# Convolution in passes of 256 channels over half the blocks, W_glu loaded in slices, and the last result made in two parts

## The chip, the core and the metric

The kernel runs on one core of a Trainium2 chip. The metric is the device time of one execution in microseconds, as the median of three runs. A profile of one further execution gives the busy times, waits and DMA packets that the text reads. Engine names are those of the profile: PE is the matrix engine (PEld is its weight load), DVE the vector engine, ACT the scalar engine, POOL the GpSimd engine, SP the engine that issues most DMAs. A queue with a q at its end (SPq, ACTq, POOLq) stands for the DMA issues of that engine.

## The reference

There are two layers on an input x of 32 images, 128 channels and 32 x 32 pixels (1024 positions), all in float32.

The first layer is a state-space block. Its input is u, the group norm of x with groups of 4 channels. For each image it computes

- h = W_enc^T u + b_enc, which has 1024 channels,
- a causal convolution of each channel of h along the 1024 positions with a filter of 64 taps, which comes from the parameters of that channel, plus D times h; the result goes through gelu and is called y,
- g = y W_glu + b_glu, which has 2048 columns, and then the first half times the sigmoid of the second half,
- the layer norm of h + g over the 1024 channels, then W_dec, which brings it back to 128 channels.

The result is added to x and gives x1.

The second layer is a deformable convolution with 64 taps (8 x 8). A depthwise 3 x 3 convolution of the group norm of x1 gives an x and a y offset for every tap and pixel. Each tap samples the normed image bilinearly at its shifted place, every channel has a weight of its own for every tap, the sum over the taps goes through a batch norm and gelu, and it is added to x1.

## The kernel before

**Filter table.** `ssm_kernel_table` builds the filters of all 1024 channels and writes them to DRAM as `kp_d`, one row of 320 values per channel, of which 64 are taps and the others zero.

**Convolution stage** (`ssm_convolution`, L183 to L341). The positions of an image are cut into 8 blocks of 128. The stage makes 8 passes of 128 channels (the loop over k at the end). A pass has two parts.

`encode(k)` makes z for all 32 images. For each image it loads u (512 KB, L236; in the first pass it makes u by the group norm of x and stores it with an ACT DMA), and does two groups of 4 matmuls that give 128 positions x 128 channels each (L223). The bias is added by DVE on the way out of PSUM (L227, 128 x 512), with a write that is strided by channel. Two PSUM buffers (`psz`) take turns.

`convolve(k, z)` takes 8 channels at a time, 16 times. For them it loads `toe` with SP (L281): 128 partitions x 8 channels x 192 values, each partition one value further along the row of the filter, so that it holds a band matrix whose outer columns are zeros. The ring has three such tiles. For each of two halves (i) of the blocks and each channel, one matmul with z as weights (4 blocks x 32 images are its 128 rows) and toe as the moving operand gives 192 columns (L299). The 64 columns that run over into the next block are copied by ACT (`t`, L307) and added to the next block's rows by DVE (`carry`, L311); the last block of the first half is carried to the second half from the tile `last`. ACT applies gelu (L320) into a `yo` tile, of which there are six; POOL stores it to `y_d` with 8 DMAs of 128 KB per 8 channels (L332). The carry is followed by `finish()`, which issues the gelu or the stores of the step before. The order is written by hand (`manual_schedule`).

**Main block** (`main_block`). It takes over the on-chip memory of the convolution stage. It loads its constants with SP (L588) and all of W_glu (8 MB, eight ACT DMAs, L597), folds the layer norm's gamma and beta into W_dec (the matmuls of L625 and L637 and the DVE scaling of L632, all in `pdec`), and clears `rel_d` with four zero stores (L653). `first_part(b)` is the rest of the first layer for an image, in two halves of 512 positions: it loads y (`gy`, L677) and u, and for m from 0 to 7 does eight matmuls for the gate (L757), the sigmoid on ACT (L764), eight for the value (L780) and then h (L796). A tile (image and half) takes some 130 us when it is alone.

`second_part(b, steps)` is the sampling of an image. The taps and columns of the image are cut into 17 packs (`PACKS`) of up to 16 slots and each pack into 4 pieces of two filter rows. Per piece, SP loads hat functions in x (`ds`) and y (`dhy`) from DRAM (`load_hat`, L1029), DVE multiplies them (L1048), and three matmuls over the row ranges of `rows_of` (L1091, windows starting at rows 0, 8 and 16) sample the image. DVE multiplies by the tap weights (L1094), POOL or DVE adds the two filter rows (L1111), POOL adds into `acc` (L1116). A pack whose slots are not one run in DRAM needs several loads (`runs_of`): four for the first and the last pack, two for the second and the last but one. `steps` are pieces of work for the next image that are placed at given counts.

`run_along` merges `first_part(b + 2)` and `second_part(b)` in proportion to estimated costs. For the last two images (from `ALONE` on) there is no first part left; the hats in x are then loaded into 32 partitions only and spread by ACT copies (L1040).

**End.** After the last pack of an image, POOL takes off the mean and scales (L1122), ACT applies gelu (L1126), DVE adds x1 (L1127) and ACT issues the store (L1128). For the last image these four come after everything else. Then `deformable_redo` compares the largest offsets with `BOUND_X` and `BOUND_Y` (L1177 to L1194) and reads the outcome back: an image whose offsets are beyond the bound would be done again by `deformable_general`, a slow general path.

Of the kernel before, what the change touches and what calls it, by code (L numbers as in the profile page):

```python
# [14 lines left out]
P = 128  # L15
# [167 lines left out]
def ssm_convolution(nc, tc, const, ins, x, u_d, kp_d, y_d):  # L183
# [7 lines left out]

    ORDER = (0, 2, 1, 3)
    NB = NJ // 2
    RW = TW - P
    QC = 4
    with tc.tile_pool(name="cvt", bufs=3) as tp, tc.tile_pool(
        name="cvz", bufs=1
    ) as zp, tc.tile_pool(name="cv1", bufs=1) as one, tc.tile_pool(
        name="cvu", bufs=5
    ) as up, tc.tile_pool(name="cvy", bufs=6) as yp, tc.tile_pool(  # L200
# [7 lines left out]
        nc.sync.dma_start(b_enc, ins["b_enc_row"].to_broadcast([P, D]))  # L208

        def encode(k):  # L210

            z = [
                pool.tile([P, P, NB, B], F32, tag=f"z{g}", name=f"z_{k}_{g}")
                for g, pool in enumerate((one, zp))
            ]
            bias = b_enc[:, k * P : (k + 1) * P]

            def image(b, u):
                for g in range(2):
                    ps = psz.tile([P, NB, P], F32, tag="ps", name=f"psz_{k}_{b}_{g}")  # L220
                    for j in range(NB):
                        lo = (NB * g + ORDER[j]) * P
                        nc.tensor.matmul(  # L223
                            ps[:, j, :], u[:, lo : lo + P], w_enc[:, k * P : (k + 1) * P],
                            start=True, stop=True,
                        )
                    nc.vector.tensor_add(  # L227
                        z[g][:, :, :, b].rearrange("p d j -> p j d"),
                        ps,
                        bias[:, None, :].to_broadcast([P, NB, P]),  # L230
                    )

            if k > 0:
                for b in range(B):
                    u = up.tile([P, L], F32, tag="u", name=f"u_{k}_{b}")
                    nc.sync.dma_start(u, u_d[b])  # L236
                    image(b, u)
                return z
# [28 lines left out]
        def convolve(k, z):  # L267
            rows = [t.rearrange("p d j b -> p d (j b)") for t in z]
            waiting = []

            def finish():
                for work in waiting:
                    work()
                waiting.clear()

            for g in range(P // CG):
                d0 = k * P + g * CG
                toe = tp.tile([P, CG, TW], F32, tag="toe", name=f"toe_{d0}")
                table = kp_d[d0 : d0 + CG, 0:TW]

                nc.sync.dma_start(  # L281
                    toe,
                    bass.AP(
                        tensor=table.tensor,
                        offset=table.offset,
                        ap=[[1, P], [KPW, CG], [1, TW]],
                    ),
                )
                yo = [
                    yp.tile([P, CG, P], F32, tag="yo", name=f"yo_{d0}_{i}") for i in range(2)  # L290
                ]
                for q in range(CG // QC):
                    c0 = q * QC
                    last = None
                    for i in range(2):
                        ps = psy.tile([P, 2, 512], F32, tag="ps", name=f"psy_{d0}_{q}_{i}")
                        ps = ps[:, :, : 2 * TW].rearrange("p h (c n) -> p h c n", c=2)
                        for c in range(QC):
                            nc.tensor.matmul(  # L299
                                ps[:, c // 2, c % 2, :],  # L300
                                rows[i][:, g * CG + c0 + c, :],
                                toe[:, c0 + c, :],
                                start=True,
                                stop=True,
                            )
                        over = tp.tile([P, 2, 2, RW], F32, tag=f"t{i}", name=f"t_{d0}_{q}_{i}")
                        nc.scalar.copy(over, ps[:, :, :, :RW])  # L307

                        def carry(to, rows, src):
                            own = ps[to : to + rows, :, :, P:TW]  # L310
                            nc.vector.tensor_add(own, own, src)  # L311

                        carry(64, 64, over[0:64])
                        carry(32, 32, over[64:96])
                        if i > 0:
                            carry(0, 32, last[96:P])
                        finish()

                        def gelu(to=yo[i][:, c0 : c0 + QC, :], ps=ps):
                            nc.scalar.activation(  # L320
                                to.rearrange("p (h c) l -> p h c l", c=2),
                                ps[:, :, :, RW:TW][:, :, :, ::-1],
                                AF.Gelu_apprx_tanh,
                            )

                        waiting.append(gelu)
                        last = over

                def store(yo=yo, d0=d0):
                    for i in range(2):  # L330
                        for j in range(NB):
                            nc.gpsimd.dma_start(  # L332
                                y_d[d0 : d0 + CG, :, i * NB + ORDER[j], :].rearrange(
                                    "d b l -> b d l"
                                ),
                                yo[i][j * B : (j + 1) * B],
                            )

                waiting.append(store)
            finish()  # L340


        with tc.manual_schedule():
            for k in range(KD):
                convolve(k, encode(k))
# [156 lines left out]
BOUND_X, BOUND_Y = 2.45, 3.25  # L502
# [9 lines left out]
def rows_of(piece):  # L512

    a, b = 15 - KY2 * piece, 23 - KY2 * piece
    return (0, a), (a, b - a), (b, H - b)
# [30 lines left out]
def main_block(nc, tc, const, ins, x, u_d, y_d, x1_d, out, offmax):  # L546
# [21 lines left out]
    with ctx:  # L568
# [27 lines left out]
        for k in range(KD):  # L596
            nc.scalar.dma_start(w_glu[:, k, :], ins["W_glu"][k * P : (k + 1) * P, :])  # L597
# [13 lines left out]
        minus = constant("minus", [P, 16])  # L611
        off_w = constant("offset_w", [P, 9])
# [8 lines left out]


        fold = pdec.tile([P, T], F32, tag="dec", name="g_fold")
        for k in range(KD):
            nc.tensor.matmul(  # L625
                fold[:, 0:1], w_dec[:, k, :], beta[:, k : k + 1],
                start=(k == 0), stop=(k == KD - 1),
            )
        shift = one.tile([P, 1], F32, tag="shift", name="g_shift")
        nc.vector.tensor_add(shift, fold[:, 0:1], b_dec)  # L630
        for k in range(KD):
            nc.vector.tensor_scalar(  # L632
                w_dec[:, k, :], w_dec[:, k, :], gamma[:, k : k + 1], None, op0=ALU.mult
# [684 lines left out]
```

## Time and profile before

| | us |
|---|---|
| median of three runs (13580.38 to 13586.92) | 13584.75 |
| the profiled execution | 13588.92 |
| its span in the profile | 13587.2 |
| PE busy (96%) | 13106.8 |
| POOL busy (67%) | 9080.3 |
| DVE busy (65%) | 8781.8 |
| ACT busy (24%) | 3291.8 |
| psy matmuls L299, 4096 rows | 704.7 |
| psz matmuls L223, 4096 rows | 568.6 |
| DVE adds for z, L227, 512 | 516.2 |
| store issues for y_d on POOL, L332, 1024 | 590.1 |

A row of the page counts a float32 matmul twice, since it is done in two rows. Busy time of PE is not PE at its peak. The span is shorter than the execution's own time by what lies before its first and after its last instruction (1.7 us). The trace also has every DMA packet with its queue, size and time; a packet of 4096 B on the POOL queue is a piece of a store of y, one of 768 B on SP's queue in the convolution stage is a row of toe.

### The profile page before, as it was taken

Reading aid. Unit: us, or ns where it says so; the run is one execution under the profiler, and the core shown is the slowest. Engines: PE = TensorE matmul, PEld = TensorE weight load, DVE = VectorE, ACT = ScalarE, POOL = GpSimd, SP = SyncE. Lnnn points to the kernel's source line nnn. Section 1 sums busy time; section 2 is a strip of 40 time slices with the busy share of each in tenths; the row PEclk is TensorE's granted clock in tenths of the full one; section 3 lists DMA queues with packets and bytes.
Section 4 is the critical chain, followed back from the end, with each engine's and each line's share of the span. In section 5 each row is a group of like instructions: output and inputs, shape, how many; then the busy total and the mean of one; then the engine's idle time right before and its main releaser. Section 6 shows DMA issues by size and latency. Waiting matters only on the chain.

```text
span 13587.2 us, 133930 instructions
## 1 busy us (share of the span) xinstructions
PE 13106.8 (96%) x40482; PEld 7248.5 (53%) x40482; DVE 8781.8 (65%) x12685; ACT 3291.8 (24%) x4767; POOL 9080.3 (67%) x8868
## 2 busy tenths in 40 slices
PE   7999899999999999999999999999999999999975
PEld 7888545555555555555555555555555555555533
DVE  7787226666666666666666666666666666666677
ACT  4333222222211122222222211112222222221145
POOL 2444227777777777777777777777777777777778
PEclk9999999999999999999999999999999999999988
DMA  7888428888888888888889888888888888988876
GB/s 244 275 277 273 132 90 231 234 239 236 231 227 231 233 235 238 238 236 232 230 234 239 235 229 229 231 232 237 238 237 236 232 230 235 240 235 231 230 198 175
DMA packets 1715626, 3105.77 MB, mean 229 GB/s; under 512 B 308306, under 2 KB 1018322, under 8 KB 1713874
## 3 DMA queue, kind: packets, MB, share of 16 engines
q1 hardware_dynamic: 1502290, 2641.91, 73.2%
q10 hardware_dynamic: 163456, 320.92, 6.6%
q0 software_dynamic: 49152, 134.28, 2.9%
q8 instruction: 329, 5.39, 0.2%
q14 instruction: 399, 3.27, 0.1%
HBM read 2630.36 MB, written 466.06 MB: 228 GB/s over the span
## 4 chain that ended last, share of the span: by engine, by line
PE 81%; DMA 9%; DVE 4%; ACT 2%; POOL 2%; issue 1%; SPq 1%; ACTq 0%; DVEq 0%; POOLq 0%
PE gpv L780 24%; PE gpg L757 23%; PE dps L1091 23%; DMA ds<-dhat 4%; PE gph L796 3%; PE gpo L685 3%; PE psy L299 3%; PE psz L223 2%; DMA y_d<-yo 2%; DMA dhat<-dh 2%; DVE z L227 1%; DVE ds L1048 1%; DMA dhy<-dhat 1%; POOL y_d L332 1%; ACT ds L1040 0%
## 5 line engine op out<-in xcount | busy, mean ns | idle before, releaser
L1094 DVE TENSOR_TENSOR dp<-dps,k_weight_slots 128x256 f32<-128x256 f32 (+17 forms) x6528 | 3087.1, 483 | 3109.5 <-PE dps L1091 2914.8
L1091 PE MATMUL dps<-ds,dxw 128*128 128x256 f32 (+18 forms) x13056 | 4701.1, 447 | 223.5 <-DVE ds L1048 177.5
L1116 POOL TENSOR_TENSOR dacc<-dacc,dp 128x256 f32<-128x256 f32 (+3 forms) x4736 | 4417.4, 933 | 396.5 <-DVE dp L1111 26.6
L1091 PEld LDWEIGHTS dps<-ds,dxw 128*128 128x128 f32 x13056 | 2472.7, 192 | 3203.6 <-issue 2537.5
L757 PE MATMUL gpg<-gy,g_w_glu 128*128 128x512 f32 x8192 | 3986.4, 593 | 23.5 <-DMA gy<-y_d 15.7
L780 PE MATMUL gpv<-gy,g_w_glu 128*128 128x512 f32 x8192 | 3975.7, 592 | 0.0
L1111 POOL TENSOR_TENSOR dp<-dp 128x448 f32<-128x448 f32 (+2 forms) x2142 | 2675.1, 1249 | 1882.1 <-DVE dp L1094 1879.4
L1048 DVE TENSOR_TENSOR ds<-ds,dhy 128x1024 f32<-128x1024 f32 (+3 forms) x2176 | 3148.6, 1447 | 762.4 <-DMA ds<-dhat 647.9
L757 PEld LDWEIGHTS gpg<-gy,g_w_glu 128*128 128x128 f32 x8192 | 1546.9, 190 | 1235.8 <-issue 964.9
L780 PEld LDWEIGHTS gpv<-gy,g_w_glu 128*128 128x128 f32 x8192 | 1551.7, 190 | 1155.3 <-issue 913.8
L818 POOL TENSOR_TENSOR gs<-gs,gq 128x512 f32<-128x512 f32 x448 | 628.5, 1403 | 1341.3 <-ACT gq L817 1341.3
L817 ACT ACTIVATE gq<-gr 128x512 f32<-128x512 f32 x448 | 282.3, 630 | 4673.6 <-DVE gr L809 4611.2
L332 POOL DMA_DIRECT2D y_d<-yo x1024 | 590.1, 583 | 869.7 <-ACT yo L320 699.2
L764 ACT ACTIVATE gs<-gpg,k_b_glu 128x512 f32<-128x512 f32 x512 | 351.8, 687 | 2488.0 <-PE gpg L757 2377.6
L953 ACT ACTIVATE dh<-dr,k_minus 128x624 f32<-128x624 f32 x768 | 621.7, 809 | 642.5 <-DMA dhat<-dh 563.1
L299 PE MATMUL psy<-toe,z 128*128 128x192 f32 x4096 | 704.7, 333 | 45.2 <-ACT yo L320 43.8
L299 PEld LDWEIGHTS psy<-toe,z 128*128 128x128 f32 x4096 | 667.5, 192 | 81.6 <-ACT yo L320 74.5
L311 DVE TENSOR_TENSOR psy<-psy,t 32x256 f32<-32x256 f32 (+1 forms) x1280 | 553.7, 433 | 204.7 <-ACT t L307 162.6
L788 DVE SCALAR_TENSOR_TENSOR gs<-gpv,k_b_glu,gs 128x512 f32<-128x512 f32 x512 | 379.7, 742 | 437.3 <-PE gpv L780 437.2
L687 POOL TENSOR_TENSOR gs<-gs,gr 128x512 f32<-128x512 f32 x448 | 634.7, 1417 | 0.0
L954 ACT ACTIVATE dh<-dh,one 128x624 f32<-128x624 f32 x768 | 626.3, 815 | 25.0
L223 PE MATMUL psz<-w_enc,u 128*128 128x128 f32 x4096 | 568.6, 293 | 44.9 <-DVE z L227 32.3
(162 smaller groups left out, 6052.4 us busy)
## 6 DMA issues: line engine op xcount, KB each, us to landing
dhy<-dhat SPq DMA_DIRECT2D x1536, 512.0 KB
ds<-dhat SPq DMA_DIRECT2D x1440, 512.0 KB
dhat<-dh ACTq DMA_DIRECT2D x768, 312.0 KB
y_d<-yo POOLq DMA_DIRECT2D x1024, 128.0 KB, 5.4
gy<-y_d SPq DMA_DIRECT2D x512, 256.0 KB
u<-u_d SPq DMA_DIRECT2D x224, 512.0 KB
toe<-kp_d SPq DMA_DIRECT2D x128, 768.0 KB
dxw<-dvt_d SPq DMA_DIRECT2D x1248, 64.0 KB
```

Of the source, the lines that this page charges most:

```text
L223: nc.tensor.matmul(ps[:, j, :], u[:, lo : lo + P], w_enc[:, k * P : (k + 1) * P], start=True, stop=True,)
L299: nc.tensor.matmul(ps[:, c // 2, c % 2, :], rows[i][:, g * CG + c0 + c, :], toe[:, c0 + c, :], start=True, stop=True,)
L332: nc.gpsimd.dma_start(y_d[d0 : d0 + CG, :, i * NB + ORDER[j], :].rearrange("d b l -> b d l"), yo[i][j * B : (j + 1) * B],)
L687: nc.gpsimd.tensor_add(sums[0], sums[0], r)
L757: nc.tensor.matmul(gate, w_glu[:, k, D + m * P : D + m * P + P], ys[k], start=(k == 0), stop=(k == KD - 1),)
L780: nc.tensor.matmul(val, w_glu[:, k, m * P : m * P + P], ys[k], start=(k == 0), stop=(k == KD - 1),)
L818: nc.gpsimd.tensor_add(sums[1], sums[1], sq)
L1048: nc.vector.tensor_mul(s[:, :m], s[:, :m], hy[:, :m])
L1091: nc.tensor.matmul(ps, xw[:, j, :], s[:, :m, :, y0 : y0 + ny], start=True, stop=True)
L1094: nc.vector.tensor_mul(prod[:, :m, :, y0 : y0 + ny], ps, w[:, :, :, None].to_broadcast([P, m, KY2, ny]),)
L1111: adder.tensor_add(prod[:, :m, 0], prod[:, :m, 0], prod[:, :m, 1])
L1116: nc.gpsimd.tensor_add(to, to, prod[:, slot : slot + nj, 0])
```

## The change

- **Passes.** A pass has 256 channels (`ZC`) and half of the blocks; there are four passes over k with two halves each. `encode(k, half)` loads half of u per image (256 KB), does two groups of two matmuls with 256 columns, and, except in the very first pass, gives every fourth group to ACT (copy) and POOL (bias) in place of DVE.
- **Convolve.** One half per pass, 32 groups of 8 channels. The three toe tiles are static and are zeroed once; only the 128 columns that can be non-zero are loaded, by two DMAs of 64 partitions each. What runs over from the first half into the second goes through DRAM (`edges`): POOL stores it in the first half, SP loads it in the second. There are five `yo` tiles for six, each stored by four DMAs.
- **W_glu.** It is loaded in slices of 128 columns, the first two pairs around the loads of the first tile, and then pair m + 2 after the sigmoid of step m of that tile, on ACT's queue. The folding of the norm moves into step m = 1 of the first tile, the clearing of `rel_d` into the part that runs along with the second image.
- **Last result.** For the last image, columns 0 to 23 are finished (on DVE, ACT, DVE) within the last pack, and the other eight columns after it. The flags of the general path are made at step 60 of the last image.
- **hy loads.** For the last two images, packs with several runs load `dhy` with ACT's queue instead of SP's (96 DMAs).
- **Rows.** `rows_of` cuts the rows of a piece as 14+9+9, 12+9+11, 10+9+13 and 9+9+14 where it was 15+8+9, 13+8+11, 11+8+13 and 9+8+15, and `BOUND_Y` goes from 3.25 to 2.25.

The core of the diff:

```diff
+        toes = []
+        for i in range(NTOE):
+            toe = one.tile([P, CG, TW], F32, tag=f"toe{i}", name=f"toe{i}")
+            nc.gpsimd.memset(toe, 0.0)
+            toes.append(toe)
+
+        def encode(k, half):
+
+            z = one.tile([P, ZC, NB, B], F32, tag="z", name=f"z_{k}_{half}")
+            chans = slice(k * ZC, (k + 1) * ZC)
...
+                for g in range(NB // 2):
+                    ps = psz.tile([P, 2, ZC], F32, tag="ps", name=f"psz_{k}_{half}_{b}_{g}")
+                    for j in range(2):
+                        lo = ORDER[2 * g + j] * P
                         nc.tensor.matmul(
-                            ps[:, j, :], u[:, lo : lo + P], w_enc[:, k * P : (k + 1) * P],
+                            ps[:, j, :], u[:, lo : lo + P], w_enc[:, chans],
                             start=True, stop=True,
                         )
...
+                    if (k > 0 or half > 0) and (2 * b + g) % 4 == 3:
+                        nc.scalar.copy(to, ps)
+                        nc.gpsimd.tensor_add(to, to, bias)
+                    else:
+                        nc.vector.tensor_add(to, ps, bias)
...
-                    u = up.tile([P, L], F32, tag="u", name=f"u_{k}_{b}")
-                    nc.sync.dma_start(u, u_d[b])
+                    u = up.tile([P, NB * P], F32, tag="u", name=f"u_{k}_{half}_{b}")
+                    nc.sync.dma_start(u, u_d[b, :, half * NB * P : (half + 1) * NB * P])
...
+            for g in range(ZC // CG):
+                d0 = k * ZC + g * CG
+                toe = toes[g % NTOE]
+
+                table = kp_d[d0 : d0 + CG, TW - P : TW]
+                for r in (0, 64):
+                    nc.sync.dma_start(
+                        toe[r : r + 64, :, 64 - r : 64 - r + P],
+                        bass.AP(
+                            tensor=table.tensor,
+                            offset=table.offset,
+                            ap=[[1, 64], [KPW, CG], [1, P]],
+                        ),
+                    )
+                if half > 0:
+                    edge = tp.tile([B, 2, 2, 2, RW], F32, tag="edge", name=f"edge_{d0}")
+                    nc.sync.dma_start(edge.rearrange("b q h c l -> b (q h c l)"), edges[g])
+                over = tp.tile([P, 2, 2, 2, RW], F32, tag="over", name=f"t_{d0}_{half}")
...
+                    if half == 0:
+                        nc.gpsimd.dma_start(
+                            edges[g], over[96:P].rearrange("b q h c l -> b (q h c l)")
+                        )
...
-    a, b = 15 - KY2 * piece, 23 - KY2 * piece
-    return (0, a), (a, b - a), (b, H - b)
+    a = (14, 12, 10, 9)[piece]
+    return (0, a), (a, 9), (a + 9, H - a - 9)
...
-        for k in range(KD):
-            nc.scalar.dma_start(w_glu[:, k, :], ins["W_glu"][k * P : (k + 1) * P, :])
+
+        def load_glu(m):
+
+            if m < KD:
+                for lo in (D + m * P, m * P):
+                    nc.scalar.dma_start(
+                        w_glu[:, :, lo : lo + P],
+                        ins["W_glu"].rearrange("(k p) n -> p k n", p=P)[:, :, lo : lo + P],
+                    )
...
                 if n == 0:
+                    load_glu(0)
                     load(0, range(KD))
+                    load_glu(1)
...
+                    if n == 0:
+                        load_glu(m + 2)
                     if m == 1:
                         load(n + 1, range(YB - KD))
+                        if n == 0:
+                            fold_norm()
...
-                nc.sync.dma_start(
+                queue = nc.scalar if a == 1 and b >= ALONE and len(runs_of(n)) > 1 else nc.sync
+                queue.dma_start(
...
+                if b == B - 1 and n == EARLY:
+                    o = two.tile([P, L], F32, tag="img", name=f"do_{b}")
+                    xr = two.tile([P, L], F32, tag="img", name=f"dxr_{b}")
+                    nc.sync.dma_start(xr, x1_d[b])
+                    steps = result(o, xr, acc, 0, SPLIT, 3 * PIECES * (n + 1))
+            if b == B - 1:
+                ending.extend(result(o, xr, acc, SPLIT, W, 0))
+                ending.append((9, lambda: nc.scalar.dma_start(out[b], o)))
+                return
...
+                (start + 6, lambda: nc.vector.tensor_scalar(
+                    part(o), acc[:, x0:x1], bn_mean, bn_inv,
+                    op0=ALU.subtract, op1=ALU.mult,
+                )),
+                (start + 7, lambda: nc.scalar.activation(
+                    part(o), part(o), AF.Gelu, bias=bn_beta
+                )),
+                (start + 12, lambda: nc.vector.tensor_add(part(o), part(o), part(xr))),
```

## The prediction

> **What bounds the kernel now.** I read the page's slices first: PE is busy at 9 tenths nearly everywhere, but the first four and a half slices are the convolution and the last two run the last images without a partner, and these are the stretches that the change edits. So I cut them out with the busy time by stretch (columns: stretch, its us, then busy us of PE, weight loads, DVE, ACT, POOL, then PE clock, DMA share, GB/s).
>
> ```profile
> 512.00:610.00 98.00, 91.30 (x535) 86.56 (x534) 71.33 (x161) 55.59 (x126) 63.88 (x111) 0.98 0.88 283
> 610.00:680.00 70.00, 64.71 (x484) 57.84 (x484) 61.98 (x63) 1.44 (x4) 9.81 (x18) 1.00 0.84 258
> ```
>
> The first line is one convolve of 128 channels, the second one encode. In the chain of waits, convolves begin at 514.66 and 683.88; the one between ends at 611.76. So a convolve takes 97 us, an encode 72 us here (on average 70: the stage runs from 183.25 to 1448.2, 1265 = 8 x 97 + 7 x 70). In a convolve PE needs 512 rows x 0.170 us (19.07 us for 112 rows in the chain) = 87 us. The other 10 us are in the chain, which over 505 to 700 us is 17% stores of y:
>
> ```profile
> 538.79 7.92 DMA y_d<-yo
> 546.72 0.28 issue
> 547.00 5.44 DMA y_d<-yo
> ...
> 615.13 1.17 PE psz L223 x8
> 616.32 1.04 DVE z L227
> 617.37 0.04 issue
> 617.41 1.17 PE psz L223 x8
> ```
>
> The reader is to see two different limits. The convolve waits for store completions. The DMA view of 530 to 612 us says why: nearly full in every slice.
>
> ```profile
> DMA  9899899998998998997999967999998999999998
> ```
>
> The encode alternates PE 1.17 and DVE 1.05 over two PSUM buffers, 2.29 us for two groups; 64 groups are 73 us. DMA is not its limit: u is fetched at the pace of use.
>
> The trace's DMA packets, sorted by queue and size, price the convolve (524 to 611 us): toe packets of 768 B took 44 ns on average (median 36), store packets of 4096 B 185 ns (median 173). A group of 8 channels needs 1024 toe packets and 256 store packets over 16 engines: 2.82 + 2.96 = 5.8 us of every engine, against 32 PE rows x 0.170 = 5.4 us. So DMA already sets the convolve's pace.
>
> Then the two ends of the main block, from the timeline:
>
> ```profile
> 1437.28 10.88 PE L299 MATMUL psy<-toe,z 128*128 128x192 f32 x64 [0.61 <-ACT yo L320]
> ...
> 1476.98 1.92 SPq L653 DMA_DIRECT2D rel_d<-zero  x4
> ...
> 1479.79 11.59 SPq L677 DMA_DIRECT2D gy<-y_d  x8
> 1491.28 5.46 PE L757 MATMUL gpg<-gy,g_w_glu 128*128 128x512 f32 x6 [15.70 <-DMA gy<-y_d]
> ```
>
> ```profile
> 13571.28 4.64 POOL L1122 TENSOR_SCALAR do<-dacc,k_bn_mean,k_bn_var 128x1024 f32<-128x1024 f32 x1
> 13575.95 1.15 ACT L1126 ACTIVATE do<-do,k_bn_beta 128x1024 f32<-128x1024 f32 x1 [12.75 <-POOL do L1122]
> 13577.12 1.23 DVE L1127 TENSOR_TENSOR do<-do,dxr 128x1024 f32<-128x1024 f32 x1 [8.01 <-ACT do L1126]
> 13578.38 0.34 ACTq L1128 DMA_DIRECT2D out<-do  x1
> ```
>
> PE's gap between the stages is 1448.2 to 1491.3, 43 us; after the last accumulation the tail is 13571.2 to 13587.2, 16 us.
>
> **What the Trainium skill says.** "DMA: Bandwidth & Descriptors", Specifications, puts the smallest transfer for line rate at 512 B; the new toe packets have just that. The trace agrees: 512 B packets of dxw in the main block took 27 ns at the median, 768 B 36, 2048 B 84, so about 8 ns are fixed, and 512 B carry 19.0 B/ns against 21.3. "SBUF — State Buffer", Door 1, says that 64 partitions in one half reach 8 of 16 ports (196 GB/s against 328 at 1 MiB). The new toe loads are of that kind; no run shown has one. The DMA page, "Issuing engines are not separate DMA queues": moving a DMA to another engine saves only its issue. The hy loads moved to ACT can gain no more than that.
>
> **The change, part by part.**
>
> *Encode* (8 passes as before, now 256 channels and 4 blocks). A group is 2 matmuls of 256 columns. PE's 128x512 rows are spaced 0.43 us in the timeline, so a 256-column row is 0.215 and four are 0.86; with the 0.1 us that a fill has beyond its rows now, 0.96 against 1.17. DVE stays 1.05 a group, and every fourth group goes to ACT and POOL. Even groups all stay on DVE, so their buffer's loop is 2 x (1.05 + 0.96 + 0.07) = 4.16 us for four groups: 16 x 4.16 = 67 us. The ACT copy (0.6 to 1.0: the 128x512 rows on ACT are 0.6, the strided write may cost what it costs DVE) hides in that loop. The last group of a pass is an ACT-and-POOL one and the convolve waits for it: POOL's add is 1.4 us (L818) to 3, twice that for strides, so +1 to +4 over DVE's; I take +2. Encode 69, against 70: 7 x -1 = -7 us. The first encode, bound by its normalisation, I leave as it is; the xt ring of 5 for 6 still leads by three images. u's bytes halve, but in a stretch where DMA was not the limit.
>
> *Convolve.* PE's rows are the same (256 matmuls, 87 us). Stores are the same bytes. Toe grows: 32 groups a pass of 1024 packets of 512 B, 16.8 MB for 12.6. Edges add 32 packets of 2048 B a group (written in the first half, read in the second), 0.17 to 0.22 us. Per group: toe 1024 x 27 to 33 ns / 16 = 1.73 to 2.11 (33 scales the 44/36 seen under load), stores 128 x 173 to 185 / 16 = 1.38 to 1.48; sum 3.3 to 3.8 us, and PE needs 2.72. So DMA bounds it at either end. Over 32 groups 105 to 122; less three toes prefetched (5 to 6) and five yo tiles stored after the end (7); plus about 3 before the first store: 96 to 112, at 95% occupancy up to 117. If the half-port loads cost 10% more, 4 more. I take 107: +10 x 8 = +80 us. Below nothing it reaches about -1 a pass. POOL issues 160 DMAs in a first half, 160 x 0.575 = 92 us: covered. The over ring (three tiles) now waits for the edge store to land (5.4 us after issue, some 10 after the copy): 3.3 us a group, also covered; without that cover it would be the pace. The toe ring leads by two groups, now 5.4 us at PE's pace; a toe took 2.2 us from first to last packet alone and 4.7 to 6.9 among stores, so at that pace it would be just late, at DMA's pace it isn't. SP carries two toe issues and an edge per group, 1.1 us of 3.3: covered. The memsets of three toes lie beside the filter table.
>
> *The gap.* In the built program each DMA of SP and ACT waits for the one that used its completion semaphore, of eight in turn. W_glu's 8 MB no longer hold these up for SP's constants, and the four zero stores move behind. The constants then take about 11 us (0.45 each), so gy waits for y's last stores only (issued until 1462.8 now, landing near 1469, T+21 from PE's last row). First matmul at about T+23 instead of T+43: -20. The folding of the norm, which lay in that gap (1468.16 to 1475.8), moves between matmuls of the first tile: +7.5. Net -13 (ends -20 and -3). The later slices, 1 MB per 17 us, lie in a stretch at 0.09 DMA share; they are issued on ACT behind a sigmoid and nothing there is late. Clearing rel_d moves past SP's loads of tile 1, 1.9 us in a stretch with room.
>
> *The tail.* After the last accumulation only a quarter is left: about 0.4 + 0.5 + 0.4 instead of 7.1 us, -5.8. The flag work after the out issue (13579.10 to 13580.38 and the reads behind it) has been done at step 60: about -2.5. The first 24 columns now cost DVE some 1.5 us inside the last pack. Net -7 (-12 to -3).
>
> *hy on ACT* for the two last images: 96 issues of 0.62 us move from SP to ACT. In the last pack SP is full (13536 to 13560: 2.48 + 2.62 us a piece), so 2.5 us a piece are freed; but ACT then has 2.5 of issue, waiting for DVE's multiply, ahead of 1.9 of copies that the next multiply waits for: 1.1 + 2.5 + 1.9 = 5.5 a piece against about 5.1. Zero, +-10.
>
> *Rows and bound.* Same columns per piece (14+9+9 for 15+8+9), so PE and DVE sums stand: 0. The largest vertical offset that the reference's inputs give is 2.10, under 2.25; the general path stays skipped.
>
> Sum: -7 + 80 - 13 - 7 = +53. The profiled execution took 13588.92 (span 13587.2), 4 above the median; the parts are differences, so I add them to the median: 13584.75 + 53 = 13638.
>
> **Rivals.** (1) DMA-bound convolve, as worked out: 13600 to 13700. For it: the DMA line above. Chance 0.50. (2) Balance, ending faster or the same: total bytes per pass fall (u -8.4, toe +4.2, edges +2 MB), and if packets run at their medians a convolve is 96 and an encode 65 (POOL's tail hidden): 8 x -1 + 7 x -5 = -43, with gap and tail -63: 13522; its middle course, convolve 100, gives 13550 to 13612. It decides for the other side as soon as a convolve takes under 98 us. For it: stalls may come per time and not per packet. Against: 44 ns is the mean under just this load. Chance 0.17 for its faster end, 0.20 for its middle. (3) Half-port loads or the edge ring set a pace of 4 us a group: convolve 120, 8 x 23 - 27 = +157: 13742. For it: the skill's table; against: half the engines' time is stores, which use other packets. Chance 0.13.
>
> **How the numbers follow.** About 0.2% (27 us) is what a measurement of this kernel tells from no change. Likeliest 13638. Faster 0.17 (rival 2's end), same 0.21 (its middle and the first case's edge), slower 0.62. The range leaves out half of the faster end and the tail of the third: 13535 to 13745; the first case alone is 13600 to 13700.
>
> **What would show it.** Right: convolves of 103 to 112 us with DMA at 9 tenths throughout and PE waiting on toe or y stores; encodes of 67 to 70; 512 B packets near 32 ns; the gap near 23 us plus fold matmuls inside the first tile; a tail under 9 us. Wrong: a convolve under 98 (packets cheaper than 28 ns, or stores draining into the encode), an encode held by POOL, or first halves much slower than second ones, which would be the edge ring.

## The result and the profile after

The changed kernel takes 13801.49 us (median of 4 runs, 13796.67 to 13803.7) against 13582.74 beside it: a ratio of 1.0159, with a 95% interval of 1.0146 to 1.0172. It is 219 us slower, where 53 were forecast, and lies above the range. In the profile the span grew from 13587.2 to 13797.9 us, by 210.7.

First the same two stretches as before, one convolve (now 256 channels, one half; at 120.0 us the longest of the eight, whose mean is 115.8) and one encode. The columns are those of the view before: stretch, its us, busy us of PE, weight loads, DVE, ACT and POOL, PE clock, DMA share, GB/s.

```profile
575.00:695.00 120.00, 94.93 (x514) 87.72 (x515) 54.93 (x126) 54.50 (x126) 84.11 (x149) 0.96 1.00 282
695.00:771.00 76.00, 64.33 (x256) 43.05 (x254) 51.85 (x50) 17.14 (x19) 32.21 (x27) 1.00 0.49 139
```

The reader is to see that the rate of bytes in the convolve is what it was (282 GB/s for 283) while the stretch is a fifth longer, with DMA at 1.00 of its time; and that the encode got no shorter, although DMA's share fell from 0.84 to 0.49. The work that the change saves was saved in a stretch that had room; the work that it adds went to the one that had none. The equal rate is no ceiling of DMA, though: the run with the whole toe below moves more. The DMA view of 595 to 690 us is full in every slice:

```profile
DMA  9999999998999999999999999999999999999999
```

What PE waited for before these matmuls is in the group's line (count, busy us, mean ns, then idle us before it and what ended it), first before the change, then after it:

```profile
L299 PE MATMUL psy<-toe,z 128*128 128x192 f32 x4096 | 704.7, 333 | 45.2 <-ACT yo L320 43.8 <-issue 0.6
L309 PE MATMUL psy<-toe,z 128*128 128x192 f32 x4096 | 750.8, 340 | 196.6 <-DMA toe<-kp_d 143.5 <-ACT yo L329 21.9 <-POOL z L237 19.5
```

Before, PE was idle for 45.2 us, nearly all of it behind gelus that waited for stores; now toe itself is what PE waits for, 143.5 us.

The chain of waits shows the encode and its end:

```profile
518.84 1.05 DVE z L239
519.93 1.15 PE psz L229 x4
521.10 1.50 DVE z L239
522.64 1.15 PE psz L229 x4
...
568.22 1.80 POOL z L237
570.02 3.10 issue
573.16 1.63 POOL z L237
574.83 4.56 PE psy L309 x16
```

Filling a PSUM buffer with 256-column rows takes 1.15 us, against 1.17 with the old ones, and eight or nine of the 48 additions that DVE makes in an encode take 1.50 us for 1.05. After the last matmul of the encode the chain runs through POOL's last additions before the convolve may start.

The gap between the stages, in the timeline:

```profile
1663.93 2.84 PE L309 MATMUL psy<-toe,z 128*128 128x192 f32 x16 [0.79 <-DMA toe<-kp_d]
...
1688.68 3.65 SPq L705 DMA_DIRECT2D gy<-y_d  x8
...
1691.49 8.65 PE L787 MATMUL gpg<-gy,g_w_glu 128*128 128x512 f32 x16 [24.73 <-DMA gy<-y_d]
```

and the tail:

```profile
13786.13 3.91 POOL L1167 TENSOR_TENSOR dacc<-dacc,dp 128x160 f32<-128x160 f32 x8
13790.08 0.50 DVE L1201 TENSOR_SCALAR do<-dacc,k_bn_mean,k_bn_var 128x256 f32<-128x256 f32 x1 [5.74 <-POOL dacc L1167]
13790.61 0.74 ACT L1205 ACTIVATE do<-do,k_bn_beta 128x256 f32<-128x256 f32 x1 [12.74 <-DVE do L1201]
13791.39 0.66 DVE L1208 TENSOR_TENSOR do<-do,dxr 128x256 f32<-128x256 f32 x1 [0.81 <-ACT do L1205]
13792.08 0.35 ACTq L1176 DMA_DIRECT2D out<-do  x1
```

Both ends are shorter, as forecast: 24.7 us for 43.1, and 2 us from the last accumulation to the issue of the result for 7.

With the first and last matmul of each stage taken from the trace, the whole difference can be laid out. An image is counted between the first matmuls of two neighbouring images of `second_part`; images 0 to 29 run beside other work or before the stage with none.

| stretch | before, us | after, us | difference |
|---|---|---|---|
| end of the first encode | 177.7 | 187.3 | +9.6 |
| eight convolves, mean of one | 93.6 | 115.8 | +178 |
| seven encodes with the wait behind them, mean of one | 74.6 | 79.0 | +31 |
| gap to the main block | 43.1 | 24.7 | -18 |
| first image of the first layer | 251.0 | 257.5 | +6.5 |
| from there to image 30, in all | | | -20 |
| image 30 | 278.4 | 300.7 | +22 |
| image 31 | 243.3 | 250.1 | +7 |
| from its last matmul to the end | 20.3 | 15.3 | -5 |
| sum | | | +211 |

### The profile page after: what moved, and what is told of

Read it like the earlier page. It is cut to its first block, busy times and chain, and to the rows that moved or that the text cites. A ratio compares the mean times of both kernels' runs of the same rounds, so it can differ in the third digit from the quotient of the medians.

```text
span 13797.9 us, 131121 instructions
## 1 busy us (share of the span) xinstructions
PE 13064.0 (95%) x38434; PEld 7118.7 (52%) x38434; DVE 8667.8 (63%) x12575; ACT 3411.9 (25%) x4880; POOL 9429.5 (68%) x9110
## 4 chain that ended last, share of the span: by engine, by line
PE 80%; DMA 10%; DVE 4%; POOL 2%; ACT 1%; issue 1%; SPq 1%; ACTq 0%; DVEq 0%; POOLq 0%
PE gpg L787 24%; PE gpv L814 23%; PE dps L1142 22%; DMA ds<-dhat 4%; DMA toe<-kp_d 3%; PE gph L830 3%; PE gpo L713 3%; PE psy L309 2%; PE psz L229 2%; DVE z L239 2%; DVE ds L1083 1%; DMA dhy<-dhat 1%; ACT ds L1075 1%; POOL dacc L1167 1%; DMA dhat<-dh 0%
## 5 line engine op out<-in xcount | busy, mean ns | idle before, releaser
L1145 DVE TENSOR_TENSOR dp<-dps,k_weight_slots 128x288 f32<-128x288 f32 (+14 forms) x6528 | 3097.2, 483 | 3237.7 <-PE dps L1142 3050.5
L1142 PE MATMUL dps<-ds,dxw 128*128 128x288 f32 (+20 forms) x13056 | 4626.6, 441 | 255.2 <-DVE ds L1083 204.4
L1167 POOL TENSOR_TENSOR dacc<-dacc,dp 128x256 f32<-128x256 f32 (+3 forms) x4736 | 4463.5, 942 | 403.9 <-DVE dp L1162 33.9
L787 PE MATMUL gpg<-gy,g_w_glu 128*128 128x512 f32 x8192 | 3993.1, 594 | 36.0 <-DMA gy<-y_d 24.7
L1083 DVE TENSOR_TENSOR ds<-ds,dhy 128x1024 f32<-128x1024 f32 (+3 forms) x2176 | 3121.8, 1435 | 712.4 <-DMA ds<-dhat 570.8
L309 PE MATMUL psy<-toe,z 128*128 128x192 f32 x4096 | 750.8, 340 | 196.6 <-DMA toe<-kp_d 143.5
L320 DVE TENSOR_TENSOR psy<-psy,t 64x256 f32<-64x256 f32 (+1 forms) x1024 | 446.3, 436 | 395.3 <-ACT t L316 371.5
L715 POOL TENSOR_TENSOR gs<-gs,gr 128x512 f32<-128x512 f32 x448 | 664.2, 1482 | 0.0
L229 PE MATMUL psz<-w_enc,u 128*128 128x256 f32 x2048 | 536.5, 406 | 102.3 <-DVE z L239 81.5
```

Of the source, the lines that this page charges most:

```text
L229: nc.tensor.matmul(ps[:, j, :], u[:, lo : lo + P], w_enc[:, chans], start=True, stop=True,)
L309: nc.tensor.matmul(ps[:, c // 2, c % 2, :], rows[:, g * CG + c0 + c, :], toe[:, c0 + c, :], start=True, stop=True,)
L715: nc.gpsimd.tensor_add(sums[0], sums[0], r)
L787: nc.tensor.matmul(gate, w_glu[:, k, D + m * P : D + m * P + P], ys[k], start=(k == 0), stop=(k == KD - 1),)
L1083: nc.vector.tensor_mul(s[:, :m], s[:, :m], hy[:, :m])
L1142: nc.tensor.matmul(ps, xw[:, j, :], s[:, :m, :, y0 : y0 + ny], start=True, stop=True)
```

## The experiments

The stretches below are read in the same way from each run's own trace. Times of single runs are given where a stretch, and not the whole, decides. How far such stretches vary: in the five kernels that have the changed convolution and encode as they are, or moved by one allocation or by the zeroing, the mean convolve is 114.4 to 115.8 us.

**The convolution stage of before in the changed kernel** (`ssm_convolution` taken over whole).

> The changed kernel with the convolution stage of the kernel before. Theory (the loss is the convolution stage alone, +219 us from first to last of its matmuls, and the rest gives 8 back): about 13583, within 15 us of the kernel before; its main block starts some 18 us earlier than there. Rival (the stage before shapes what the main block meets, so the loss does not come off whole): over 13610.

13588.1 us (12 runs), a ratio of 1.0003 to the kernel before, interval 0.9994 to 1.0012. Its convolves are 93.3 us, its encodes 74.3, the main block starts at 1473.5 for 1491.2, the first image again takes 6 us more and image 30 301.1. So the loss as a whole comes off with this stage, and the rest of the change is a draw: what gap, tail and rows gain is lost again in the first image and the last two.

**Hat loads on SP again.**

```diff
-                queue = nc.scalar if a == 1 and b >= ALONE and len(runs_of(n)) > 1 else nc.sync
+                queue = nc.sync
```

> The changed kernel with all hat loads on SP's queue again. Theory (the ACT issues stand ahead of the copies that the next multiply waits for): the last two images take 278 and 243 us again for 301 and 250, so 29 us less, 13772. Rival (the new row split costs the last images): no change there, 13800. Rival two (the finishing of 24 columns in the last pack): only the last image stays at 250.

13762.73 us, 39 less than the changed kernel. Image 30 takes 278.7 us and image 31 248.2, and the end 11.7 after its last matmul. That is 28 us; another 6 came by a convolution stage that was shorter in this profile. The cost is in the packs during which ACT issues the loads for the last two: counted from 0, packs 14 and 15 of image 30 take 22.4 and 22.2 us in the changed kernel and 16.3 and 12.7 here. In image 31 the same two packs lose 18 us, but its first and last pack get 12 of them back. The timeline of the changed kernel shows the loop:

```profile
13747.13 1.56 DVE L1083 TENSOR_TENSOR ds<-ds,dhy 128x832 f32<-128x832 f32 x1 [1.19 <-ACT ds L1075]
...
13748.72 2.70 ACTq L1064 DMA_DIRECT2D dhy<-dhat  x4
...
13751.52 1.80 ACT L1075 COPY ds<-ds 32x832 f32<-32x832 f32 x2 [4.42 <-DMA dhy<-dhat]
13753.35 1.02 DVE L1083 TENSOR_TENSOR ds<-ds,dhy 128x832 f32<-128x832 f32 x1 [2.59 <-ACT ds L1075]
```

The four issues wait on ACT for DVE's multiply (L1083), which frees the tile that they fill; the copies for the next piece stand behind them; and the next multiply waits for the copies, 6.2 us after the one before. What is left of image 31's +7 (5 us) lies in two places. The last pack, in which 24 columns are finished, takes 19.1 us for 17.1. The last piece of pack 4, after which the flags of the general path are made, takes 6.1 us for 2.5: the flags' matmul stands in PE's queue ahead of the next samples and waits 3.97 us for DVE. With the tail (-9) these parts of the change are worth 4 us here; in the last kernel of this section, which has them too, image 31 takes 244.9 us, so it is 7 there.

**The old row split and bound** (`rows_of` and `BOUND_Y` as before).

> The changed kernel with the old row split (15+8+9) and bound. Theory (the new split is what makes the images 2 to 29 faster by 0.7 us each in the profile): 20 us more, 13820. Rival (that drift comes from elsewhere, the split is worth nothing): 13801, and the images stay at their new 367.4 us mean. Rival two (the split also costs the last two images): these fall back to 278 and 243.

13812.85 us, 11 more than the changed kernel, and the intervals of the two ratios overlap (1.0151 to 1.0185 here). The stretches tell more: images 0 to 28 take 368.28 us each for 367.48, which is 23 us in 29 images, while image 30 and 31 stay at 299.3 and 251.5, so the split does not touch these. This profile's convolution stage was 11 us shorter, which hides half of it in the total. Other runs' traces agree: images 0 to 28 take 368.1 to 368.3 us in the three kernels with the old split and 367.2 to 367.8 in ten with the new one. The engine is PE. In the traces of images 2 to 27, a sampling row over 8 window rows (8 x 32 = 256 columns) is followed by the next after 235 ns (median), or 0.92 ns a column; over 9 window rows it is 249 to 250 ns for 288 columns, 0.87 ns a column, and from 10 rows on 0.84 to 0.86. The new split has no window of 8 rows. Summed over an image, PE's sampling takes 113.0 us in the changed kernel, 114.5 in this run and 114.7 before, and about half of that difference shows in the image's time.

**All additions of the encode on DVE.**

```diff
-                    if (k > 0 or half > 0) and (2 * b + g) % 4 == 3:
+                    if False:
```

> The changed kernel with every bias addition of the encode on DVE. Theory (the encode's pace is the loop of one PSUM buffer, fill 1.15 us and addition 1.05, and the POOL addition holds one DVE addition in four for 0.45 us more and delays the convolve by 2.8): an encode of 72 to 74 us with no gap behind it for 76.3 + 2.8, so 35 to 50 us less in all. Rival (DVE is the limit and the share given away pays): an encode of 80 or more and a slower run.

13752.18 us in one run, 49 less. Encodes take 73.2 us for 76.2, and the wait behind them is 1.2 us for 2.8, which makes 32 us in seven. The convolves took 113.0 us for 115.8, a little less than in any other run with this convolve; why is open. The pace of the encode in this run's timeline is two groups in 2.26 us, without a long one among them:

```profile
541.24 2.03 DVE L239 TENSOR_TENSOR z<-psz,b_enc 128x512 f32<-128x512 f32 x2 [0.23 <-PE psz L229]
543.50 2.02 DVE L239 TENSOR_TENSOR z<-psz,b_enc 128x512 f32<-128x512 f32 x2 [0.24 <-PE psz L229]
545.76 2.03 DVE L239 TENSOR_TENSOR z<-psz,b_enc 128x512 f32<-128x512 f32 x2 [0.24 <-PE psz L229]
```

So giving a quarter of the work away cost time. What the encode waits for is the loop of a PSUM buffer, fill and addition in turn, of which DVE's addition is only a part.

**The whole toe in one DMA, as before** (128 partitions, 192 columns, 768 B packets, in the new passes).

> The changed kernel with the toe load of before: one DMA of all 128 partitions and all 192 columns, in packets of 768 B. Theory (DMA bytes and packets set the convolve's pace): toe is 1024 x 44 ns / 16 = 2.8 us a group, with the stores 4.3 for 3.6, so a convolve of 125 to 138 us for 115. Rival (loads into half of the partitions are what is slow): a convolve under 115, although it moves half as many bytes again.

A convolve takes 125.3 us, 13868.11 in all. Half as many bytes again for toe, and 10 us more, at the lower end of what bytes alone ask for. From 10 us after its first matmul to 5 us before its end, a convolve here moves 345 GB/s on average; the changed kernel moves 305 in the same stretch and the kernel before 310. So "DMA is full" doesn't mean a fixed rate of bytes.

**As many packets of 512 B, but over all partitions.**

```diff
-                for r in (0, 64):
-                    nc.sync.dma_start(
-                        toe[r : r + 64, :, 64 - r : 64 - r + P],
+                nc.sync.dma_start(
+                        toe[:, :, 0:P],
...
-                            ap=[[1, 64], [KPW, CG], [1, P]],
+                            ap=[[1, P], [KPW, CG], [1, P]],
```

> The changed kernel with the same number of toe packets of 512 B, but in one DMA over all 128 partitions (columns 0 to 127 of the band are filled and the rest stays zero, so the convolution's values are not the reference's). Theory (packets and bytes): a convolve of 112 to 116 as now, packets of 31 to 33 ns. Rival (half of the partitions, half of the ports, or two DMAs a group to issue and to wait for): a convolve of 100 to 106.

A convolve takes 109.3 us, between the two: 112.4 in first halves and 106.2 in second ones, for 117 and 115 in the changed kernel. What PE waits for has changed too: it is the gelus behind the stores as much as toe.

```profile
L309 PE MATMUL psy<-toe,z 128*128 128x192 f32 x4096 | 730.7, 336 | 164.5 <-ACT yo L329 71.5 <-DMA toe<-kp_d 65.4 <-POOL z L237 19.6
```

In the stretch described above, toe packets of 512 B take 29.7 ns on average for 31.0, stores 176 for 202. So the form of the loads, two DMAs into half of the partitions each, is worth about 6.5 of the 22 us, and against this run the whole toe of the one above costs 16. Whether it is the halves or the number of DMAs, this run alone doesn't tell.

**Half of the toe loads.**

```diff
-                for r in (0, 64):
+                for r in (0,):
```

> The changed kernel with only the first of the two toe DMAs of each group (partitions 64 to 127 stay zero, so the convolution's values are not the reference's). Theory (the toe traffic, doubled per channel, is what holds PE): about 1 us of 3.6 a group goes, PE's 2.72 becomes the pace, a convolve of 88 to 95. Rival (the stores, the over ring or POOL's issues set the pace): 105 or more.

A convolve takes 97.4 us: 100.5 in first halves, 94.3 in second ones. (The run as a whole, 14922 us, says nothing: with such values of the convolution the offsets pass the bound and the general path is entered.) PE's idle time before these matmuls falls from 196.6 to 74 us, and what is left of the waits names the next limit. The two lines are those of PE's matmuls and of ACT's copies into the over tile in this run:

```profile
L309 PE MATMUL psy<-toe,z 128*128 128x192 f32 x4096 | 725.9, 336 | 74.0 <-ACT yo L329 39.4 <-POOL z L237 19.6 <-DMA toe<-kp_d 9.4
L316 ACT COPY t<-psy 128x256 f32<-128x256 f32 x512 | 190.9, 373 | 299.5 <-PE psy L309 176.7 <-DMA edges<-t 116.7 <-ACT yo L329 5.0
```

The toe traffic is the first limit; behind it, in first halves only, the over ring that waits for the edge stores, at 100 us a convolve. The five yo tiles and POOL's issues are as in the changed kernel, so neither of these holds a convolve at 115 us.

**No edges.** The store and the load are taken out; the second half adds rows of its own over tile.

> The changed kernel without the edges: neither stored nor loaded, the second half adds rows of its own over tile in their place (so the first positions of the second half are not the reference's). Theory (edges are only some more packets): 0.2 us of 3.6 a group, a convolve of 107 to 113. Rival (ACT waits for the edge store before it may write an over tile again, and this loop sets the pace of the first halves): first halves below 100, second halves as now.

109.4 us a convolve for 115.8, 109.4 in first and 109.5 in second halves, which is 7 and 5 us less, so both gain. PE still waits 114.3 us for toe. The edges act as traffic while toe is the limit, not as a ring.

**Toe tiles zeroed after the first encode.**

> The changed kernel with the three toe tiles zeroed after the first encode. Theory (the zeroing waits for the store of the filter table, whose memory the toe tiles take, and the first encode's matmuls wait behind it): the first encode ends at 178 us as before the change for 187, so 9 us less, about 13790. Rival (the first encode is slower because of the ring of five): it still ends at 187.

The first encode ends at 186.3 us for 187.3 (13812.33 us in all, in one run), so the zeroing is not the cause. The encode's matmuls started at the same time without the zeroing ahead of them. What both runs share is SP's order: the weights of the encode are issued after the store of the filter table, at 47.6 us, and at 5.05 before. In the changed kernel:

```profile
41.80 0.39 SPq L158 DMA_DIRECT2D kp_d<-kp  x1
47.66 0.34 SPq L210 DMA_DIRECT2D w_enc<-in_W_enc  x1
```

**z in a pool of its own, ahead of the weights.**

```diff
-        name="cvd", bufs=2, space=DRAM
-    ) as dram, tc.tile_pool(name="cv1", bufs=1) as one, tc.tile_pool(
+        name="cvd", bufs=2, space=DRAM
+    ) as dram, tc.tile_pool(name="cvz", bufs=1) as zp, tc.tile_pool(
+        name="cv1", bufs=1
+    ) as one, tc.tile_pool(
```

> The changed kernel with z in a pool of its own ahead of the pool of the encode's weights, as before the change, so that these weights no longer lie in memory of the filter table and SP can load them at 5 us instead of 47.7, after the table's store. Theory (this late load is what delays the first encode): its matmuls start near 31 us for 52 and it ends at 178 for 187; 9 us less, about 13792. Rival (the ring of five xt tiles): the loads are early, and it ends at 185 or later all the same.

The weights are issued at 5.05 us, and the first encode ends at 179.5. In SP's timeline of this run:

```profile
5.05 0.43 SPq L212 DMA_DIRECT2D w_enc<-in_W_enc  x1
5.53 0.43 SPq L214 DMA_DIRECT2D b_enc<-in_b_enc_row  x1
6.00 33.43 SPq L265 DMA_DIRECT2D xt<-in_x  x7
41.37 0.39 SPq L158 DMA_DIRECT2D kp_d<-kp  x1
```

So the order of the pools is the cause. That the weights, with z and them in one pool, came to lie where the filter table still was, so that their load had to wait for its store, is the likely way; the trace has the order of the issues but no addresses. 13788.11 us, 13 less. The ring of five has little part in it: 1.8 us are left to the 177.7 of before.

**The passes before with the trimmed toe alone.** Into the kernel before go the static toe tiles, zeroed after the first encode, and these two loads in place of the one of 192 columns:

```diff
+                toe = toes[g % 3]
+                table = kp_d[d0 : d0 + CG, TW - P : TW]
+                for r in (0, 64):
+                    nc.sync.dma_start(
+                        toe[r : r + 64, :, 64 - r : 64 - r + P],
```

> The kernel before with one part of the change alone: static toe tiles of which only the 128 columns that can be non-zero are loaded, by two DMAs of 64 partitions. Passes and stores are as before. Theory (the convolve before was held by DMA at 5.8 us a group against PE's 5.45; now toe is 1.9 to 2.1 and the stores 3.0, 4.9 to 5.1): PE is the pace, a convolve of 88 to 90 us for 93.6, so 30 to 45 us less, about 13545. Rival (the stores' completions hold PE whatever toe costs, or the loads into half of the partitions cost what they save): 92 to 95 a convolve, 13583.

13537.05 us (6 runs), a ratio of 0.9967, interval 0.9954 to 0.9979. A convolve takes 87.1 us for 93.6, which is PE's own time, and PE's idle time before its matmuls is 4.8 us for 45.2 in the whole stage. One convolve and one encode of this run:

```profile
499.00:586.00 87.00, 85.77 (x511) 81.39 (x512) 68.30 (x154) 54.26 (x121) 61.44 (x107) 1.00 0.87 258
586.00:660.00 74.00, 68.11 (x508) 61.38 (x507) 64.72 (x70) 3.26 (x8) 12.26 (x22) 1.00 0.82 263
```

The same loads into half of the partitions that hold PE up in the new passes don't hold it up here, since each group of toe serves two halves: 1024 packets in 5.45 us of PE's work and not in 2.72.

One thing they do here as well. With all runs side by side (mean of a store packet of 4096 B in the convolves, and the packets' times as a share of the 16 engines' time, which passes 1 where packets overlap):

| toe loads | runs | store packet, ns | share |
|---|---|---|---|
| 128 partitions, 768 B | before; old stage in the changed kernel | 182, 183 | 0.96, 0.97 |
| 128 partitions, new passes | whole toe; 512 B | 176, 176 | 1.04, 1.02 |
| two of 64 partitions, new passes | the changed kernel and six more | 199 to 203 | 1.06 |
| one of 64 partitions, new passes | half of the toe loads | 213 | 0.95 |
| two of 64 partitions, old passes | this run; the last kernel | 202, 207 | 0.95, 0.96 |

The dear stores go with loads into half of the partitions. They don't go with how busy DMA is, and not with two DMAs for one, since the half toe has one.

**What holds, together.** The last kernel adds to this the sliced W_glu, the new rows, the result in two parts and the early flags, leaves the hat loads on SP and puts the folding ahead of the first matmul:

```diff
-                        if n == 0:
-                            fold_norm()
...
                     load_glu(1)
+                    fold_norm()
```

> The passes before with the trimmed toe, and of the change the sliced W_glu, the row split, the finishing in two parts and the early flags; the hat loads stay on SP and the folding of the norm is back in the gap ahead of the first tile. Theory: convolve -5 x 8, gap -16, rows -20, last image and tail -2 to -4, no fold inside the first tile: about 13505. Rival (the fold, waiting for its constants, holds the first matmul): 13512.

13498.49 us (4 runs), a ratio of 0.994, interval 0.9924 to 0.9957: 84 us less than the kernel before and 303 less than the changed one. The gap is 26.6 us and the first image 249.8, so the folding costs no more than the 2 us by which this gap is longer. In the gap:

```profile
1421.42 3.54 PE L665 MATMUL g_fold<-k_ln_beta,k_W_dec 128*128 128x1 f32 x16 [17.81 <-DMA k_ln_beta<-in_ln_beta]
...
1425.51 3.58 PE L676 MATMUL g_fold<-g_ones,k_W_dec 128*128 128x1 f32 x16 [0.54 <-DVE k_W_dec L671]
...
1430.20 2.05 PE L782 MATMUL gpg<-gy,g_w_glu 128*128 128x512 f32 x2 [1.11 <-DMA gy<-y_d]
```

The first matmul still waits for y at the end, by 1.1 us, and not for the fold.

## Why the prediction was wrong

The side was right and so was the mechanism of the likeliest case: a convolve bound by DMA through its toe loads. The half of toe (-18 us a convolve), the whole toe (+10) and the trimmed toe in the old passes (-6.5) show it. What failed are sizes in the sum: the convolve, for which 107 us were taken, and with it the encode, the hat loads on ACT, and two terms that were put at nothing.

*Convolve: +178 for +80.* Two steps are in these 98 us. The first is the base: "a convolve takes 97 us, an encode 72 us here (on average 70" was read from one convolve (95.1 us from first to last matmul) and the start of the encode behind it. The means before are 93.6 and 74.6. That is 27 us in eight convolves; the total of the stage was right, so the encode's difference is off the other way.

The second is the level: 115.8 for "I take 107", 70 us in eight. The step had 3.3 to 3.8 us a group, from toe packets at 27 to 33 ns and stores at 173 to 185. In the changed kernel they took 31.0 and 202 ns, edge loads 97: 1.98 + 1.61 + 0.2 = 3.8 us, the upper end. What had been left out of the 107 is the loads by halves: "If the half-port loads cost 10% more, 4 more". The run over all partitions put them at 6.5 us, and without them a convolve took 109.3, close to 107. Their cost sits mostly in another term of the sum, the stores. These had been priced beside loads into 128 partitions, where they take 182 ns; beside loads into 64 they take 202. The step did scale toe for the load it would meet, but it took stores at their old price. (Since DMA was busy throughout the stretch, the mean times of its packets add up to about the time that passed, whatever made it long. That 3.8 us a group fit is therefore no second proof; the proof is in the runs that change the loads.)

The Trainium skill's statement on 64 partitions ("SBUF — State Buffer", Door 1: 196 GB/s for 328) points to the right side. The 6.5 of 116 us seen here are much less, among stores that use DMA's time as well.

*Encode: +31 for -7.* In levels it was 79.0 us, with the wait behind it, for 69. "0.96 against 1.17" for a fill was wrong: measured, it is 1.15. The new rows start 0.216 us apart, as the step has it; what was wrong is "the 0.1 us that a fill has beyond its rows now". The eight old rows start 0.112 us apart, 0.9 us in all, so the old fill has 0.27 us beyond them, and the new one has as much (0.29). Longer rows could save next to nothing. With 1.15 the loop of a buffer is 2 x (1.15 + 1.05 + 0.07) = 4.5 us for four groups, 73 us an encode, and this is what the run with all additions on DVE showed (73.2). The second part is the help of POOL: eight or nine additions of DVE's 48 took 1.50 us for 1.05 while an addition of POOL's ran, which is the other 3 us of the 76.2; and the last addition delayed the convolve by 2.8, where +2 was taken. "The encode alternates PE 1.17 and DVE 1.05 over two PSUM buffers" was right; that a third engine could only help was not.

*First encode: +9.6 for 0.* "The first encode ... I leave as it is" looked at engines and rings and not at the order in which tiles are given memory. The zeroing of toe, which stood ahead of the matmuls in the waits of PE by name, was the wrong suspect too; pool order was the cause.

*hy on ACT: +28 for 0 +- 10.* The loop was written down ("5.5 a piece against about 5.1"), but it was set against SP's busy time in the last pack alone. The loads for a pack are issued four pieces ahead, so they fall into the pack before it, where SP was not the limit. In packs 14 to 16 of image 30, pieces take 5.6 to 5.7 us, as the 5.5 had it, where they take 3.2 to 4.8 with the loads on SP.

*Gap and fold: -12 for -13* (-18.4 and +6.5), right by its steps. *Tail: -4 to -7 for -7*, with the hat loads on SP: -9 after the last matmul, and +5 in one run and +2 in another before it. "Some 1.5 us inside the last pack" were 1 to 2; the flags at step 60, which the sum had as a gain only, held PE for some 3 us.

*Rows: -20 for 0.* "PE and DVE sums stand" holds in columns and not in time: PE took 0.92 ns a column over windows of 8 rows and 0.87 over 9, and the new split has none of 8.

The rival with a convolve of 120 us priced it nearest (13742). Of its two reasons, loads into half of the partitions were real, at 6.5 us a convolve and not 23. The edge ring makes first halves 6 us longer than second ones in the two runs with cheaper toe loads (112 and 100 us), and 2 in the changed kernel; it sets no pace of 120.

## What to carry to other kernels

Balance a resource by stage, not by the pass: the change lowered the bytes of a pass slightly and lost 22 us a convolve, since it moved them from the encode (DMA share 0.84, then 0.49) into the convolve, where DMA was full; ask of every tile that is loaded how many us of work it serves (toe: 5.45, then 2.72). A packet's price belongs to the traffic it was measured in: a new form of load changed what the stores beside it cost. A DMA issue that has to wait holds up whatever stands behind it on the engine that issues it, as it did ACT's copies behind the hat loads. Before an engine is given a share of the work, check that the engine it relieves is what the loop waits for: here it was a PSUM buffer.

## What the runs showed of the hardware that was not expected

- Four rows of 256 columns fill a PSUM group in 1.15 us, eight rows of 128 columns in 1.17. The rows start 0.216 and 0.112 us apart, so either fill has some 0.28 us beyond them.
- DVE's addition of a PSUM group and an SBUF row took near 1.50 us for 1.03 in 60 of the 210 cases in which an addition of POOL's ran beside it in the seven later encodes, and in none of the 126 without; which of them it hits is open.
- Store packets of 4096 B averaged 176 to 183 ns beside loads into 128 partitions and 199 to 213 beside loads into 64, with DMA shares of 0.95 to 1.06. Their median hardly moved (167 to 174).
- A matmul row over windows of 8 values each (256 columns) took 235 ns, one over windows of 9 (288 columns) 249 to 250: 0.92 and 0.87 ns a column.
- A copy of 128x512 by ACT out of PSUM with the strided write took 1.03 us, as DVE's addition does, and POOL's addition 1.7.
